# A sum of squared matrix products on one core: one of seven product trees with 20 narrow products, and partial sums that stay in PSUM

## The chip, the cores and the metric

The kernel runs on one core of one Trainium2 chip. The metric is the device time of one execution in microseconds. The trace and its profile page show one execution; the times come from repeated runs without the profiler.

## What is computed

```python
def _L0_rec_ref(x, weight, lin_w, lin_b):      # x 1024x512, weight 64x512x512 (e, f, m), all fp32
    out_lin = x @ lin_w.T + lin_b
    xv = jnp.einsum('bf,efm->bem', x, weight)
    zp = jnp.einsum('bf,efm->bem', jnp.square(x), jnp.square(weight))
    interaction = 0.5 * jnp.sum(jnp.square(xv) - zp, axis=1)
    return out_lin + interaction
```

The large part is `xv`: a 1024x512 matrix times a 512x32768 matrix in fp32, whose result is squared and summed over `e`. The subtracted part needs only the sum over `e` of the squared weights and one small product at the end.

## The kernel before

**Stages.** First comes a prologue: `x` is loaded, the linear part `x @ lin_w.T` is computed (line 369), and the blocks `X1` to `X7` are formed, which are the sums and differences of blocks of `x` that a fast matrix product needs. Then the 512 columns of `m` are worked in groups: two groups of 16 columns of `m` and 20 groups of 24. At the end comes the small product with the summed squares (line 776), and the output is stored.

**A group.** A group is one product of 1024x512 by 512x(24*64) (16*64 in the first two). It is split in two along each of the three dimensions, and 7 outer products take the place of 8 (the Strassen-Winograd scheme); they run in the order 1, 6, 2, 7, 4, 5, 3. Each outer product is a *tree*: it is split in two along each dimension once more and made of 7 inner products, P1 to P7. An inner product is two matmuls (two blocks of 128 rows of `x`) with 384 columns (256 in the first two groups). Each fp32 matmul shows in the trace as two passes, so a tree is 28 passes of 384 columns, each pass with its own weight load.

**PSUM.** There are four pairs of banks: `b1`, `b3`, `b2_0`, `b2_1`. In a tree, P5 goes to `b3` and is copied by ScalarE to SBUF (tile `p5`). P3 is added onto it in `b3` and the sum is copied to SBUF too (tile `p53`). P1 goes to `b1` and is copied by ScalarE to one of the `b2` pairs; P6 is added onto the copy there, then P7, then P4, and the pair is read after each. P2 is added to P1 in `b1`. So four sums come out of a tree, at positions 0 to 3, and two of them also need `p53` or `p5`.

**The outer sums.** `outer_psum` and `outer_sbuf` (lines 518 and 530) add what comes out of PSUM onto the tiles `oa`, `ob` and `c`. In `outer_sbuf`, VectorE first adds bank and `p53` (or `p5`), and a second sum adds this in SBUF to `oa`, `ob` or `c`; that second sum can run on GpSimd or on VectorE. When a block of `xv` is whole, `finish` squares it in place on ScalarE and sums over `e` on VectorE.

**The sums of weights.** Four sums of weight blocks per tree, 128x384 each, are made by GpSimd into tiles `t` (three buffers in turn). GpSimd also issues the accumulating DMAs (line 325) that form `T1`, `T2` and the like. `w_squares` squares the weights on ScalarE and sums them on VectorE.

**The order.** The program is a list of operations with costs. `Plan.order` simulates the engines and fixes the order in which each engine runs its queue. An inner product carries a key: the start of its tree plus `PLACE` times the time of one inner product; among the products that could run, TensorE takes the one with the smallest key. An operation that may run on VectorE or on GpSimd (a sum in SBUF) is taken by VectorE only if it is due within `SPARE` = 15 us.

**The wide tree.** `wide_tree` and `widen` are in the kernel but not used, since `HK` is empty. A wide tree splits an outer product into 4 blocks of rows, 2 of the inner dimension and 3 of columns and takes 20 products in place of 24. Each is one matmul of 256 columns. It uses six single banks as partial sums: `T` and `U` (in `b1` or `b3`), `Q`, `S` (the tree's own `b2` pair), `R`, `V` (the other `b2` pair), with copies by ScalarE from one bank to another between the products.

Of the kernel before, what the change touches and what calls it, by code (L numbers as in the profile page):

```python
# [30 lines left out]
TBUF = 3  # L31
SPARE = 15.0
AHEAD = 20.0
PE, DVE, ACT, POOL, SP = "PE", "DVE", "ACT", "POOL", "SP"

# [5 lines left out]
class Plan:  # L41
# [6 lines left out]

    def add(self, costs, emit, reads=(), writes=(), key=None, land=0.0, both=False):
        op = SimpleNamespace(  # L50
            n=len(self.ops), costs=costs, emit=emit, key=key, land=land,
            deps=set(), succ=[], latest=None, end=None, both=both,
        )
# [128 lines left out]
class Reg:  # L182


    def __init__(self, tile, off, n, *outer):
        self.tile, self.off, self.n, self.outer = tile, off, n, outer
        self.size = n
        offs = [off]
# [8 lines left out]
    @property  # L197
    def ap(self):
        t = self.tile.ap
        free = [list(x) for x in self.outer] + [[1, self.n]]  # L200
        return bass.AP(tensor=t.tensor, offset=t.offset + self.off, ap=[list(t.ap[0])] + free)


@with_exitstack
def kernel(
# [22 lines left out]
    )  # L228
    ps = ctx.enter_context(
        tc.tile_pool(name="ps", bufs=1, space=bass.MemoryType.PSUM)  # L230
    )
    ctx.enter_context(tc.manual_schedule())

    buf = {}

    def make(name, size, pool=sb, unit=SEG):
        t = pool.tile([P, size], F32, tag=name, name=name)
        buf[name] = SimpleNamespace(name=name, ap=t[:, :], unit=unit, size=size, psum=pool is ps)
        return name

    def reg(name, off=0, n=None, *outer):
        t = buf[name]
        return Reg(t, off, t.size - off if n is None else n, *outer)

    def ring(names):
# [19 lines left out]
    for name in ("b1", "b3", "b2_0", "b2_1"):  # L265
        make(name, 2 * N, ps, N)
    b2_ring = ring(["b2_0", "b2_1"])
    acc_ring = ring([make(f"acc{k}", NB * max(GROUPS), sb, 4) for k in range(2)])
    make("w2_sum", NK * M, sb, 4)
    make("bias", M)  # L270
# [10 lines left out]
    def tt(o, a, b, sub=False, only=None):  # L281
# [5 lines left out]
        def emit(e):  # L287
            f = engines[e].tensor_sub if sub else engines[e].tensor_add
            f(o.ap, a.ap, b.ap)  # L289

        plan.add({e: c for e, c in costs.items() if only in (None, e)}, emit,
                 a.atoms + b.atoms, o.atoms, both=not psum)

    def copy(o, i, negative=False):
        def emit(_):
            if negative:
                nc.scalar.activation(o.ap, i.ap, AF.Copy, scale=-1.0)
            else:
                nc.scalar.copy(o.ap, i.ap)  # L299

        plan.add({ACT: 0.19 + 0.00083 * o.size}, emit, i.atoms, o.atoms)

# [28 lines left out]
    def mm(o, x, w, start, key):  # L331
# [6 lines left out]
            ],  # L338
            sum((r.atoms for r in (*x, w, *o)), ()), sum((r.atoms for r in o), ()), key=key,
        )  # L340

# [19 lines left out]
    for k in range(NK):  # L361
        q, r = divmod(k, KH)
        for g, bank in enumerate(lin_banks):
            x = x_in(g // 2, q, r)
            w = reg("ob", KH * H + k * M, M)

            def emit(_, k=k, g=g, bank=bank, x=x, w=w):
                for j in range(2):
                    nc.tensor.matmul(  # L369
                        reg(bank, j * N, N).ap, x.ap[:, ts((g * 2 + j) % (NB // 2), P)], w.ap,  # L370
                        start=(k == 0), stop=(k == NK - 1),
                    )

            plan.add({PE: 2 * mm_cost(N)}, emit, x.atoms + w.atoms, reg(bank).atoms,
                     key=-1000 + 4 * k + g)
    for g, bank in enumerate(lin_banks):
        name, off = ("c", g * 2 * M) if g < 3 else ("w22b", 0)
        for j in range(2):
            tt(reg(name, off + j * M, M), reg(bank, j * N, N), reg("bias"))
        o = reg(name, off, 2 * M)  # L380
# [106 lines left out]
    def tree(time, g, i):  # L487
# [57 lines left out]

        b2, p5, p53 = b2_ring(), p5_ring(), p53_ring()
# [16 lines left out]
    def wide_tree(time, g, i, fresh_bank):  # L563
# [9 lines left out]
        def twice(x):  # L573
            return Reg(x.tile, x.off, x.n, (0, 2))

# [15 lines left out]
        for o, a, b, sub in sums:  # L591
# [7 lines left out]
        aux = "b2_1" if main == "b2_0" else "b2_0"  # L599
        bank = {"T": (fresh, 0), "U": (fresh, 1), "Q": (main, 0), "S": (main, 1),  # L600
                "R": (aux, 0), "V": (aux, 1)}
        cost = mm_cost(V)

        def h(b, half=None):
            name, k = bank[b]
            return reg(name, k * N, 2 * V) if half is None else reg(name, k * N + half * V, V)

# [35 lines left out]
        product(17, "U", 0, True)  # L643
        copy(Reg(h("Q").tile, h("Q").off, V, (V, 2)), twice(h("U", 0)))
        product(10, "T", 1, True)
# [124 lines left out]
    out_dst = out.rearrange("(n p) m -> p n m", p=P)  # L770
    for g, bank in enumerate(("b3", "b1", "b2_0", "b2_1")):
        h = g // 2
        for j in range(2):
            def emit(_, bank=bank, g=g, h=h, j=j):
                for k in range(NK):
                    nc.tensor.matmul(  # L776
                        reg(bank, j * N, N).ap,
                        view(xe[h, k // KH])[:, k % KH, ts((g * 2 + j) % (NB // 2), P)],
                        reg("w2_sum", k * M, M).ap,
                        start=(k == 0), stop=(k == NK - 1),  # L780
                    )

            plan.add({PE: 4 * mm_cost(N)}, emit,
                     xe[h, 0].atoms + xe[h, 1].atoms + reg("w2_sum").atoms,
                     reg(bank, j * N, N).atoms, key=1e6 + 2 * g + j)
            o = Reg(acc_all[g].tile, j * M, M)
            tt(o, reg(bank, j * N, N), Reg(lin_all[g].tile, j * M, M))
            dma(out_dst[:, g * 2 + j, :], o.ap, o.atoms, ())

    for op, engine in plan.order():  # L790
        if op.emit:
            op.emit(engine)

# [32 lines left out]
```

## Time and profile before

| | |
|---|---|
| runs | 1440.97 us median of 3 (1438.86 to 1448.26) |
| profiled execution | 1446.54 us, of which the span of the trace is 1444.8 us |
| TensorE | 1422.6 us busy, 98% of the span, 4440 passes |
| VectorE | 1101.6 us busy, 76% |
| ScalarE | 786.4 us busy, 54% |
| GpSimd | 1149.3 us busy, 80% |

PE is TensorE's matmuls, PEld its weight loads, DVE VectorE, ACT ScalarE, POOL GpSimd; SP's queue issues the plain DMAs. Busy time is the union of an engine's instructions. Neighbouring instructions of one engine overlap a little in the records, so the distance between two starts is what an engine gives up for one instruction. A row "L289 POOL TENSOR_TENSOR t<-w" is the operation of line 289 that reads `w` and writes `t`; buffer numbers are left out.

### The profile page before, as it was taken

How to read it: one execution, taken by the hardware profiler on the slowest of the kernel's cores; microseconds unless marked ns; L12 is line 12 of the kernel's file. 1: busy time of each engine (PE TensorE's matmuls, PEld its weight loads, DVE VectorE, ACT ScalarE, POOL GpSimd, SP SyncE). 2: the span in 40 equal slices, each digit the busy share in tenths (PEclk: the TensorE clock that was granted, in tenths of full speed). 3: DMA queues.
4: the chain of work that ended last, by engine and by line, in shares of the span. 5: the costliest groups of instructions: out<-in, count | busy, mean ns of one | idle time of the engine just before them, and what ended most of it. 6: DMA issues, size and time to landing. Idle time of an engine off the chain costs nothing.

```text
span 1444.8 us, 14609 instructions
## 1 busy us (share of the span) xinstructions
PE 1422.6 (98%) x4440; PEld 839.8 (58%) x4440; DVE 1101.6 (76%) x1226; ACT 786.4 (54%) x1038; POOL 1149.3 (80%) x995
## 2 busy tenths in 40 slices
PE   8999999999999999999999999999999999999998
PEld 3786555555555555555555555555555555555553
DVE  2888778696968778696967869696877869687785
ACT  1456556464746546464555646474654647465541
POOL 6878688797978879796878879797887979788771
PEclk9999999999999999999999999999999999999999
DMA  7666545364555446455454536455544645554242
GB/s 237 168 137 169 131 112 134 90 165 102 138 133 123 120 101 164 90 153 118 120 129 112 134 91 164 102 140 133 123 121 101 164 90 153 123 134 110 68 137 73
DMA packets 78894, 184.53 MB, mean 128 GB/s; under 512 B 28064, under 2 KB 29088, under 8 KB 78816
## 3 DMA queue, kind: packets, MB, share of 16 engines
q1 hardware_dynamic: 65488, 115.17, 25.7%
q0 software_dynamic: 12752, 67.38, 25.4%
q10 hardware_dynamic: 576, 1.05, 0.2%
q8 instruction: 37, 0.61, 0.2%
q14 instruction: 41, 0.34, 0.1%
HBM read 127.04 MB, written 6.19 MB: 92 GB/s over the span
## 4 chain that ended last, share of the span: by engine, by line
PE 91%; DVE 4%; issue 2%; DMA 1%; POOL 1%; ACT 0%; DVEq 0%; SPq 0%; POOLq 0%; ACTq 0%
PE b L335 87%; PE b L776 2%; PE b L369 2%; DVE oa L289 1%; DVE acc L314 1%; DVE ob L289 1%; DMA T<-T1a 1%; DMA w<-T 1%; POOL t L289 0%; DVE c L289 0%; DVE X L391 0%; DMA ob<-lin_wT 0%; DVE p L289 0%; ACT p L299 0%; POOL w L325 0%
## 5 line engine op out<-in xcount | busy, mean ns | idle before, releaser
L335 PE MATMUL b<-t,X 128*128 128x384 f32 (+1 forms) x2464 | 825.9, 478 | 2.7 <-ACT p L299 1.3
L335 PEld LDWEIGHTS b<-t,X 128*128 128x128 f32 x2464 | 464.7, 190 | 317.5 <-POOL t L289 11.8
L299 ACT COPY p<-b 128x768 f32<-128x768 f32 (+1 forms) x308 | 239.2, 777 | 329.7 <-PE b L335 306.2
L335 PE MATMUL b<-w,X 128*128 128x384 f32 (+1 forms) x1056 | 370.8, 481 | 6.2 <-ACT p L299 2.2
L335 PEld LDWEIGHTS b<-w,X 128*128 128x128 f32 x1056 | 199.7, 191 | 143.8 <-DVE oa L289 16.5
L289 POOL TENSOR_TENSOR t<-w 128x384 f32<-128x384 f32 (+1 forms) x176 | 173.1, 996 | 35.6 <-PE b L335 32.9
L299 ACT COPY b<-b 128x768 f32<-128x768 f32 (+1 forms) x154 | 117.6, 764 | 147.9 <-PE b L335 145.0
L289 POOL TENSOR_TENSOR t<-w,t 128x384 f32<-128x384 f32 (+1 forms) x176 | 188.1, 1069 | 9.6 <-PE b L335 8.5
L305 ACT ACTIVATE oa<-oa 128x768 f32<-128x768 f32 (+1 forms) x176 | 140.4, 822 | 70.3 <-POOL oa L289 38.4
L314 DVE TENSOR_REDUCE w_sum<-wsq 128x12 f32<-128x768 f32 (+1 forms) x176 | 160.2, 921 | 17.8 <-ACT wsq L305 16.3
L314 DVE TENSOR_REDUCE acc<-oa 128x12 f32<-128x768 f32 (+1 forms) x176 | 158.2, 919 | 0.5 <-ACT oa L305 0.5
L289 DVE TENSOR_TENSOR p<-b,p 128x768 f32<-128x768 f32 (+1 forms) x132 | 122.4, 928 | 26.6 <-PE b L335 26.5
L289 DVE TENSOR_TENSOR ob<-b,p 128x768 f32<-128x768 f32 (+1 forms) x44 | 41.1, 933 | 116.0 <-PE b L335 112.6
L289 POOL TENSOR_TENSOR ob<-ob,oa 128x768 f32<-128x768 f32 (+1 forms) x40 | 71.8, 1795 | 65.0 <-DVE ob L289 65.0
L305 ACT ACTIVATE wsq<-w 128x768 f32<-128x768 f32 (+1 forms) x132 | 106.8, 826 | 30.1 <-DMA w<-weight 25.3
L289 DVE TENSOR_TENSOR oa<-b,p 128x768 f32<-128x768 f32 (+1 forms) x88 | 81.9, 931 | 23.3 <-PE b L335 23.3
L335 PE MATMUL b<-T,X 128*128 128x384 f32 (+1 forms) x264 | 93.5, 477 | 0.4 <-POOL t L289 0.4
L289 DVE TENSOR_TENSOR ob<-b,oa 128x768 f32<-128x768 f32 (+1 forms) x44 | 41.1, 934 | 64.7 <-PE b L335 62.4
L289 POOL TENSOR_TENSOR c<-c,oa 128x768 f32<-128x768 f32 (+1 forms) x43 | 78.5, 1826 | 9.6 <-DVE c L289 9.5
L289 POOL TENSOR_TENSOR ob<-p,ob 128x768 f32<-128x768 f32 (+1 forms) x43 | 76.5, 1779 | 10.3 <-DVE p L289 10.3
L289 POOL TENSOR_TENSOR oa<-oa,ob 128x768 f32<-128x768 f32 (+1 forms) x44 | 84.0, 1909 | 0.1
L305 ACT ACTIVATE ob<-ob 128x768 f32<-128x768 f32 (+1 forms) x88 | 72.4, 825 | 16.8 <-DVE ob L289 11.6
(85 smaller groups left out, 1651.6 us busy)
## 6 DMA issues: line engine op xcount, KB each, us to landing
w<-weight SPq DMA_DIRECT2D x120, 384.0 KB, 3.7
T<-weight SPq DMA_DIRECT2D x40, 384.0 KB, 4.4
w<-T POOLq DMA_DIRECT2D x20, 768.0 KB, 6.0
T1a<-weight SPq DMA_DIRECT2D x20, 384.0 KB, 4.3
w22a<-weight SPq DMA_DIRECT2D x20, 384.0 KB, 3.4
T1a<-weight POOLq DMA_DIRECT2D x10, 768.0 KB, 7.0
T<-T1a POOLq DMA_DIRECT2D x10, 768.0 KB, 6.0
T1b<-weight SPq DMA_DIRECT2D x20, 384.0 KB, 5.2
```

What stands on the lines that cost most here:

```text
L289: f(o.ap, a.ap, b.ap)
L299: nc.scalar.copy(o.ap, i.ap)
L305: lambda _: nc.scalar.activation(o.ap, i.ap, AF.Square), i.atoms, o.atoms)
L314: nc.vector.tensor_reduce(o, x, axis=AX.X, op=ALU.add)
L335: nc.tensor.matmul(a.ap, b.ap, w.ap, start=start, stop=True, skip_group_check=True)
L369: nc.tensor.matmul(reg(bank, j * N, N).ap, x.ap[:, ts((g * 2 + j) % (NB // 2), P)], w.ap, start=(k == 0), stop=(k == NK - 1),)
L776: nc.tensor.matmul(reg(bank, j * N, N).ap, view(xe[h, k // KH])[:, k % KH, ts((g * 2 + j) % (NB // 2), P)], reg("w2_sum", k * M, M).ap, st ...
```

## The change

- Outer product 1 of the 20 groups of 24 runs as a wide tree (`HK = (1,)`); `widen(1)` makes its 20 blocks of `X1` once, before the first of these groups.
- In the trees of products 6, 2, 7, 4 and 3 (`HOLD`) the sum of P5 and P3 isn't copied to `p53`. It stays in `b3`, and VectorE adds both banks, one after the other, onto the target (two sums with a PSUM input). The inner products of these trees have other places (`HPLACE`). This holds in all 22 groups.
- `SPARE` = -99: VectorE takes no sum that GpSimd can do. `APART`: the plan starts no GpSimd operation beside one of VectorE's sums in SBUF, and none of these beside a running GpSimd operation.
- Two of a tree's four sums of weights, `t1` and `t3`, become one GpSimd instruction over 768 columns.
- Each bank is also a tensor of its own, at the same address as its half of the pair. Wide trees and the small products use the single banks, trees the pairs; `follow` adds the waits between the two views.

```diff
-HK = ()
+HK = (1,)
 PLACE = {5: -6, 3: -2, 1: 0, 6: 3, 2: 4, 7: 6, 4: 9}
+HOLD = (6, 2, 7, 4, 3)
+HPLACE = {5: -1, 1: 0, 3: 1, 6: 2, 2: 3, 4: 11, 7: 5}
-SPARE = 15.0
+SPARE = -99.0
+APART = True
...
+            if APART and e == POOL and free[DVE] > now + 0.1 and running[DVE].both:
+                return None
...
+                if APART and o.both and e == DVE and free[POOL] > now + 0.1:
+                    continue
...
+        base = nc.psum_base
+        pair = nc.alloc_psum_tensor(name, [P, 2 * N], F32).ap()
+        top, nc.psum_base = nc.psum_base, base
+        banks = [nc.alloc_psum_tensor(f"{name}_{k}", [P, N], F32).ap() for k in "lr"]
...
-        for o, a, b in ((t[1], b12, b11), (t[2], b22, t[1]), (t[3], b22, b12), (t[4], b21, t[2])):
+        tt(reg(tn, 0, n, (2 * n, 2)), reg(r, n, n, (2 * n, 2)), reg(r, 0, n, (n, 2)), True, POOL)
+        for o, a, b in ((t[2], b22, t[1]), (t[4], b21, t[2])):
             tt(o, a, b, True, POOL)
+        hold = i in HOLD
...
-               rhs[p], first, time + PLACE[p] * pair)
+               rhs[p], first, time + (HPLACE if hold else PLACE)[p] * pair)
...
+            elif hold and p is None:
+                a, o = part(ADDEND[i], pos), part(TARGET[i], pos)
+                tt(o, whole(bank), a)
+                tt(o, o, whole("b3"))
+                if i in (2, 4, 3):
+                    end(TARGET[i], pos)
...
-        copy(small(p53), whole("b3"))
+        if not hold:
+            copy(small(p53), whole("b3"))
...
+    def follow(op, engine, made):
+        for at, write, alone in op.banks:
+            before = [written[at]] if at in written else []
+            for other, was_alone, insts in before + (read[at] if write else []):
+                if was_alone != alone and not (engine == other == PE):
+                    for x in made:
+                        for y in insts:
+                            tc.add_manual_dep(x.ins, y.ins.name, wait, reason="view of a bank")
...
```

More of the change, by code (lines that the diff above doesn't have):

```diff
@@ L47, in __init__, with add @@
         self.readers = defaultdict(list)
-    def add(self, costs, emit, reads=(), writes=(), key=None, land=0.0, both=False):
+    def add(self, costs, emit, reads=(), writes=(), key=None, land=0.0, both=False,
+            banks=()):
         op = SimpleNamespace(
             n=len(self.ops), costs=costs, emit=emit, key=key, land=land,
-            deps=set(), succ=[], latest=None, end=None, both=both,
+            deps=set(), succ=[], latest=None, end=None, both=both, banks=banks,
         )
@@ L182, with __init__ @@
 class Reg:
-    def __init__(self, tile, off, n, *outer):
+    def __init__(self, tile, off, n, *outer, alone=False):
         self.tile, self.off, self.n, self.outer = tile, off, n, outer
+        self.alone = alone
         self.size = n
@@ L198, in ap, with banks @@
     def ap(self):
-        t = self.tile.ap
+        t, off = self.tile.ap, self.off
+        if self.alone:
+            t, off = self.tile.banks[off // self.tile.unit], off % self.tile.unit
         free = [list(x) for x in self.outer] + [[1, self.n]]
-        return bass.AP(tensor=t.tensor, offset=t.offset + self.off, ap=[list(t.ap[0])] + free)
+        return bass.AP(tensor=t.tensor, offset=t.offset + off, ap=[list(t.ap[0])] + free)
+    def banks(self, written):
+        return tuple((a, written, self.alone) for a in self.atoms) if self.tile.psum else ()
 @with_exitstack
@@ L265 @@
     for name in ("b1", "b3", "b2_0", "b2_1"):
-        make(name, 2 * N, ps, N)
+        base = nc.psum_base
+        pair = nc.alloc_psum_tensor(name, [P, 2 * N], F32).ap()
+        top, nc.psum_base = nc.psum_base, base
+        banks = [nc.alloc_psum_tensor(f"{name}_{k}", [P, N], F32).ap() for k in "lr"]
+        assert nc.psum_base == top
+        buf[name] = SimpleNamespace(name=name, ap=pair, banks=banks, unit=N, size=2 * N, psum=True)
     b2_ring = ring(["b2_0", "b2_1"])
-    acc_ring = ring([make(f"acc{k}", NB * max(GROUPS), sb, 4) for k in range(2)])
-    make("w2_sum", NK * M, sb, 4)
+    acc_ring = ring([make(f"acc{k}", NB * max(GROUPS), 4) for k in range(2)])
+    make("w2_sum", NK * M, 4)
     make("bias", M)
@@ L296, in emit @@
             if negative:
[L297 to L301, printed above, removed]
+                return nc.scalar.activation(o.ap, i.ap, AF.Copy, scale=-1.0)
+            return nc.scalar.copy(o.ap, i.ap)
+        plan.add({ACT: 0.19 + 0.00083 * o.size}, emit, i.atoms, o.atoms,
+                 banks=i.banks(False) + o.banks(True))
     def square(o, i):
@@ L339, in mm @@
             sum((r.atoms for r in (*x, w, *o)), ()), sum((r.atoms for r in o), ()), key=key,
+            banks=sum((r.banks(True) for r in o), ()),
         )
@@ L362, with emit @@
         q, r = divmod(k, KH)
-        for g, bank in enumerate(lin_banks):
+        for g, b in enumerate(lin_banks):
             x = x_in(g // 2, q, r)
             w = reg("ob", KH * H + k * M, M)
-            def emit(_, k=k, g=g, bank=bank, x=x, w=w):
-                for j in range(2):
+            o = [bank(b, j) for j in range(2)]
+            def emit(_, k=k, g=g, o=o, x=x, w=w):
+                return [
                     nc.tensor.matmul(
-                        reg(bank, j * N, N).ap, x.ap[:, ts((g * 2 + j) % (NB // 2), P)], w.ap,
+                        o[j].ap, x.ap[:, ts((g * 2 + j) % (NB // 2), P)], w.ap,
                         start=(k == 0), stop=(k == NK - 1),
                     )
-            plan.add({PE: 2 * mm_cost(N)}, emit, x.atoms + w.atoms, reg(bank).atoms,
-                     key=-1000 + 4 * k + g)
-    for g, bank in enumerate(lin_banks):
+                    for j in range(2)
+                ]
+            plan.add({PE: 2 * mm_cost(N)}, emit, x.atoms + w.atoms, reg(b).atoms,
+                     key=-1000 + 4 * k + g, banks=o[0].banks(True) + o[1].banks(True))
+    for g, b in enumerate(lin_banks):
         name, off = ("c", g * 2 * M) if g < 3 else ("w22b", 0)
         for j in range(2):
-            tt(reg(name, off + j * M, M), reg(bank, j * N, N), reg("bias"))
+            tt(reg(name, off + j * M, M), bank(b, j), reg("bias"))
         o = reg(name, off, 2 * M)
@@ L544, in outer_sbuf @@
                     end(TARGET[i], pos)
-        b2, p5, p53 = b2_ring(), p5_ring(), p53_ring()
+        b2, p5, p53 = b2_ring(), p5_ring(), None if hold else p53_ring()
         product(5, "b3", True)
@@ L573, in twice @@
         def twice(x):
[L574 removed]
+            return Reg(x.tile, x.off, x.n, (0, 2), alone=x.alone)
         tn = t_ring()
@@ L643, in wide_tree @@
         product(17, "U", 0, True)
-        copy(Reg(h("Q").tile, h("Q").off, V, (V, 2)), twice(h("U", 0)))
+        copy(Reg(h("Q").tile, h("Q").off, V, (V, 2), alone=True), twice(h("U", 0)))
         product(10, "T", 1, True)
@@ L770, with emit @@
     out_dst = out.rearrange("(n p) m -> p n m", p=P)
[L771 removed]
+    for g, b in enumerate(("b3", "b1", "b2_0", "b2_1")):
         h = g // 2
         for j in range(2):
[L774 to L775 removed]
+            z = bank(b, j)
+            def emit(_, z=z, g=g, h=h, j=j):
+                return [
                     nc.tensor.matmul(
[L777 to L778 removed]
+                        z.ap, view(xe[h, k // KH])[:, k % KH, ts((g * 2 + j) % (NB // 2), P)],
                         reg("w2_sum", k * M, M).ap,
@@ L781, in emit @@
                     )
+                    for k in range(NK)
+                ]
             plan.add({PE: 4 * mm_cost(N)}, emit,
                      xe[h, 0].atoms + xe[h, 1].atoms + reg("w2_sum").atoms,
-                     reg(bank, j * N, N).atoms, key=1e6 + 2 * g + j)
+                     z.atoms, key=1e6 + 2 * g + j, banks=z.banks(True))
             o = Reg(acc_all[g].tile, j * M, M)
-            tt(o, reg(bank, j * N, N), Reg(lin_all[g].tile, j * M, M))
+            tt(o, z, Reg(lin_all[g].tile, j * M, M))
             dma(out_dst[:, g * 2 + j, :], o.ap, o.atoms, ())
+    wait = mybir.DependencyInfo(mybir.DependencyClass.Sync, mybir.DependencyReason.DATA)
+    written, read = {}, defaultdict(list)
+    def follow(op, engine, made):
[6 more added lines that the diff above has]
+                            tc.add_manual_dep(x.ins, y.ins.name, wait, reason="view of a bank")
+        for at, write, alone in op.banks:
+            if write:
+                written[at], read[at] = (engine, alone, made), []
+            else:
+                read[at].append((engine, alone, made))
     for op, engine in plan.order():
         if op.emit:
-            op.emit(engine)
+            made = op.emit(engine)
+            if op.banks:
+                follow(op, engine, made if isinstance(made, list) else [made])
 def kernel(r_x, L0_rec_weight, L0_rec_lin_w, L0_rec_lin_b):
```

22 lines of the change are left out of this document (11 added, 11 removed).

## The prediction

> **What bounds the kernel now.** I read the page first (busy times, chain), then the waits of TensorE in the long middle part, then busy time by stretch.
>
> ```profile
> span 1444.8 us, 14609 instructions
> PE 1422.6 (98%) x4440; PEld 839.8 (58%) x4440; DVE 1101.6 (76%) x1226; ACT 786.4 (54%) x1038; POOL 1149.3 (80%) x995
> ...
> PE 91%; DVE 4%; issue 2%; DMA 1%; POOL 1%; ACT 0%; DVEq 0%; SPq 0%; POOLq 0%; ACTq 0%
> ...
> engine line waited for: us in total, times, longest us
> PE b L335 <- ACT p L299: 2.2, 1, 2.2
> ...
> core 0: us, PE busy (x) PEld busy (x) DVE busy (x) ACT busy (x) POOL busy (x), PEclk, DMA share, GB/s
> 55.00:140.00 85.00, 80.39 (x344) 65.22 (x343) 70.28 (x104) 49.47 (x85) 70.19 (x79) 0.98 0.61 151
> 400.00:600.00 200.00, 199.69 (x617) 116.09 (x616) 150.99 (x165) 112.42 (x145) 162.14 (x136) 1.00 0.51 123
> 600.00:800.00 200.00, 197.52 (x604) 114.44 (x603) 153.43 (x164) 110.87 (x143) 160.74 (x135) 0.99 0.50 120
> ```
>
> TensorE is the bound: 98% of the span, 91% of the chain, and between 200 and 1390 us (the waits row) it waited once, 2.2 us. So time can come only from fewer passes, from that one wait, and from the 16-column groups, where some 5 of 85 us are idle. And every wait that the change adds at TensorE shows in full.
>
> **Fewer passes.** The pace of 384 and of 256 columns, from a group of 24 and a group of 16:
>
> ```profile
> 563.82 4.03 PE L335 MATMUL b<-t,X 128*128 128x384 f32 x12
> 567.69 1.45 PE L335 MATMUL b<-T1a,X 128*128 128x384 f32 x4
> ...
> 86.34 2.75 PE L335 MATMUL b<-t,X 128*128 128x256 f32 x12
> 88.93 1.03 PE L335 MATMUL b<-w,X 128*128 128x256 f32 x4
> ...
> L335 PEld LDWEIGHTS b<-t,X 128*128 128x128 f32 x2464 | 464.7, 190 | 317.5 <-POOL t L289 11.8 <-issue 9.1 <-DVE p L289 8.6
> ```
>
> Twelve passes take 3.87 us at 384 columns (0.3225 each) and 2.59 us at 256 (0.2158). A tree has 14 matmuls, 28 passes, 9.03 us; a wide tree 20 matmuls, 40 passes, 8.63 us. The weight load of 0.19 us still fits under a pass of 0.2158, as it does in the 16-column groups. Saved: 0.40 us in each of 20 groups, **7.9 us**. It is the whole gain that the arithmetic offers, 0.55%.
>
> **VectorE's sums in SBUF go.** Here is where the one long wait comes from:
>
> ```profile
> 701.01 5.90 DVE L289 TENSOR_TENSOR ob<-ob,p 128x768 f32<-128x768 f32 x1
> 707.00 0.80 ACT L299 COPY p<-b 128x768 f32<-128x768 f32 x1 [3.83 <-DVE ob L289]
> 707.86 2.93 PE L335 MATMUL b<-w,X 128*128 128x384 f32 x4 [2.17 <-ACT p L299]
> 710.58 1.80 PE L335 MATMUL b<-t,X 128*128 128x384 f32 x4
> ...
> L289 DVE TENSOR_TENSOR ob<-ob,p 128x768 f32<-128x768 f32 x19 | 41.8, 2199 | 0.0
> L289 DVE TENSOR_TENSOR oa<-p,oa 128x768 f32<-128x768 f32 x20 | 19.2, 959 | 2.1
> L289 POOL TENSOR_TENSOR ob<-ob,p 128x768 f32<-128x768 f32 x21 | 39.4, 1877 | 5.3 <-DVE p L289 5.3
> ```
>
> One and the same sum takes VectorE 0.96 us with GpSimd quiet and 2.2 us beside it, and once 5.90 us, while GpSimd ran sums back to back. ScalarE's copy waited behind that one, and TensorE behind the copy. Then four passes took 2.72 us (707.86 to 710.58) where they take 1.29. The stretch 600 to 800 has 604 passes where 400 to 600 has 617: 13 passes, **4.2 us**, of which 2.2 are the wait and the rest slow passes behind it. The change sends these sums to GpSimd, so the event can't happen again. But it belongs to this one execution: the profiled 1446.5 us lie 5.6 above the median of the runs, whose lowest is 2.1 below the median. A median run can hold at most about those 2.1 us of such events; I take 1.0.
>
> [...]
>
> **Load of the engines per group of 24.** VectorE: five HOLD trees each get one more sum with a PSUM input (0.95 us long, 0.87 apart), two sums in SBUF go, and tree 1's two sums of 768 become two of 512 and four of 256.
>
> ```profile
> L289 DVE TENSOR_TENSOR p<-b,p 128x768 f32<-128x768 f32 x120 | 114.2, 952 | 24.9 <-PE b L335 24.9
> L289 DVE TENSOR_TENSOR p<-b,p 128x512 f32<-128x512 f32 x12 | 8.2, 685 | 1.6 <-PE b L335 1.6
> L299 ACT COPY b<-b 128x768 f32<-128x768 f32 x140 | 109.6, 783 | 139.1 <-PE b L335 139.1
> L299 ACT COPY b<-b 128x512 f32<-128x512 f32 x14 | 8.0, 571 | 8.8 <-PE b L335 5.9 <-DVE c L289 1.0 <-DVE oa L289 0.8
> L289 POOL TENSOR_TENSOR t<-w 128x384 f32<-128x384 f32 x160 | 158.9, 1005 | 31.1 <-PE b L335 30.2 <-POOL t L289 0.8
> L289 POOL TENSOR_TENSOR ob<-p,ob 128x512 f32<-128x512 f32 x3 | 3.8, 1273 | 0.2 <-DVE p L289 0.2
> L289 POOL TENSOR_TENSOR t<-w 128x256 f32<-128x256 f32 x16 | 14.2, 910 | 4.5 <-PE b L335 2.6 <-DMA w<-T 1.9
> ```
>
> A step of 256 columns is worth 0.27 us on VectorE and 0.21 on ScalarE, so I estimate 0.41 and 0.36 for 256. VectorE: +4.4 -3.2 -1.7 +2.9 = +2.4 us on 48 (76% of 63.2; it becomes 80%). ScalarE: -5 x 0.80 for the copies to `p53`, and tree 1's five copies (4.0) become six of 512 and five of 256 (5.2): -2.8. GpSimd: twelve outer sums become nine (-5.5); 28 sums of weights (28) become six trees of one 768 sum (as `ob<-ob,p`, 1.88) and two of 384 (23.3), and wide sums of 4 x 1.27 + 4 x 0.91 = 8.7: +4.0. In all -1.5. No engine becomes the bound by its load. What's left are waits at single places.
>
> **HOLD trees: shorter turns through ScalarE.** By `HPLACE` P5, P1, P3, P6 stand in a row, so that one product (1.29 us) lies between P5 and P3 and between P1 and P6, where the old places leave several; P3 must wait until P5 is copied, P6 until P1 is. The end of the program shows a turn with one product between:
>
> ```profile
> 1408.98 2.74 PE L335 MATMUL b<-t,X 128*128 128x384 f32 x8
> 1409.18 0.78 ACT L299 COPY b<-b 128x768 f32<-128x768 f32 x1 [3.02 <-PE b L335]
> 1410.02 1.09 PEld L335 LDWEIGHTS b<-t,X 128*128 128x128 f32 x4 [0.20 <-ACT b L299]
> ```
>
> The copy began 0.20 us after the product, and the load for the next one waited for it, yet the eight passes ran without a gap (2.74 us is 8 x 0.3225 plus the end of the last). 1.04 us from product to load, 0.19 for the load, 1.29 to hide it: it fits by 0.06 us if ScalarE is free. If a square is in its way (0.84 us) up to 0.8 is lost, in 110 trees up to 86 us; but P4 of the tree before (key 11) is at hand to fill, which gives 0. A gain is excluded: TensorE waited for such a copy only once. The copies to `p53` would be free of cost anyway, since ScalarE is busy 54%; their going gives it room. `b3` is now held until VectorE's second sum, some 2.1 us after P6; P5 of the next tree comes three products later. I take the end at 0, with **1 us** in all.
>
> **The wide tree's own turns.** Three: 17 is copied to `Q` before 19 and 7 (cover 0.86 us, two products; needed 0.20 + 0.57 + 0.25 = 1.02); 3, a VectorE sum and a copy to `V` before 11 (cover 2.2, needed 1.7); 2 and the reads of `S` before 13 (cover 0.86, needed 1.1 or more). Uncovered that is 0.4 us per tree, 8 us in all, the same as the saving; covered by P4 of tree 3 and P5, P1, P3 of tree 6, which have other banks, it's 0. The fillers are four products (5 us), so I stay near 0: **1.5 us**.
>
> **GpSimd ahead of the wide tree.** Rows of one group, from outer product 5 to 1:
>
> ```profile
> 566.24 1.97 POOL L289 TENSOR_TENSOR t<-w 128x384 f32<-128x384 f32 x2
> ...
> 569.01 1.82 POOL L289 TENSOR_TENSOR oa<-oa,p 128x768 f32<-128x768 f32 x1
> 570.79 1.82 POOL L289 TENSOR_TENSOR ob<-ob,p 128x768 f32<-128x768 f32 x1
> 572.87 1.81 POOL L289 TENSOR_TENSOR oa<-oa,p 128x768 f32<-128x768 f32 x1 [0.27 <-DVE p L289]
> ...
> 578.01 1.45 PE L335 MATMUL b<-w,X 128*128 128x384 f32 x4
> ```
>
> Most of tree 1's sums were made here (up to 568) before tree 5's additions (569 on), and the fourth of these additions was one of the VectorE sums that go. After: their buffer `t` is free only once tree 4's P4 has run, two products later than before (key 11 for 9), so the wide sums (8.7 us) meet four additions (7.3) between 569 and tree 1's start: P3 at 578.0, P1 two products later, at 580.6, where product 17 would stand. That is 16.0 us of work in 11.6: 4.4 us late, if the additions go first; 0 if those to `oa`, which tree 1 writes only some 5 us after its start, go behind. Behind a late sum stand the wide tree's products and then tree 6's, which share its banks. The plan orders by due time, so I stay near 0: **1.5 us** over 20 groups.
>
> **The rest.** In the prologue two sums of 1024 and the 13 operations of `widen` (some 7 us) come to GpSimd, in the narrow groups HOLD trims its work; the transitions' waits are between operations that depend on each other anyway. I take 0 for these, between -3 and +4.
>
> **The sum.** Against the profiled execution (1446.5, 1.7 outside the span): 1446.5 - 7.9 - 4.2 + 1 + 1.5 + 1.5 = 1438.4. Against the median, which is 5.6 lower and holds less of the stall: 1440.97 - 7.9 - 1.0 + 4.0 = 1436.1. I predict **1436**, and 1431 to 1441 for this case.
>
> **Rivals.** (a) *The gain comes whole*: the turns all hide, and the narrow groups win back 2 of their 5 us: 1441 - 7.9 - 1 - 2 = 1430. For it: TensorE had one wait in 1190 us. Against: the shorter cover. (b) *Slower: GpSimd late for the wide tree.* One mechanism: TensorE stands at product 17 or 10 of tree 1 until its sums are there. It decides from 0.45 us per group (20 x 0.45 = the gain of 8.9). At 1.3 us it gives 1441 - 8.9 + 26 = 1458. Waits of 2 us also bring slow passes behind them, as at 707.86. For it: the 16 us above, and no more help by VectorE. Against: 80% average load, falling. [...] (c) *HOLD's copies meet a busy ScalarE*: 110 trees x 0.15 = 16, so 1441 - 8.9 + 16 = 1448. (d) *No shorter pace*: in the wide tree every second pass carries a wait, so loads stop running ahead: 40 x (0.19 + 0.06) = 10.0 us, 1.0 more than a tree, +20: 1441 - 1 + 20 = 1460. Against: the narrow groups' pace.
>
> **How the numbers follow.** Forecast 0.50, (a) 0.20, (b) 0.18, (c) 0.08, (d) 0.04. A measurement here can tell about 1%, 14.4 us, from no change. Faster by more needs 1426.6: a fifth of (a), 0.04. Slower by more needs 1455.4: two thirds of (b), a quarter of (c), three quarters of (d), 0.17. Within 1%: 0.79. The range runs from 1428 (every cost 0, 2.1 of waits gone and 3 won back: 1441 - 7.9 - 2.1 - 3) to 1456 ((b) at 1.2 us per group).
>
> **What would show it.** Right: 240 more passes (12 in each of 20 trees), those of tree 1 at about 0.216 us; groups of 24 some 62.8 us apart instead of 63.2; no VectorE sum `ob<-ob,p`; copies `p<-b` of 768 down from 280 to 140 (five HOLD trees lose one each, tree 1 two); waits of TensorE in the middle part of some 4 us in all. Wrong: TensorE waiting on `POOL t` at each tree 1 (b), on `ACT p` or `ACT b` in the HOLD trees (c), passes of 256 at 0.25 (d).

## The result and the profile after

| | before | after |
|---|---|---|
| median of the runs | 1441.09 us (4 runs, 1438.86 to 1448.26) | 1426.93 us (4 runs, 1426.46 to 1427.61) |
| profiled execution | 1446.54 us, span 1444.8 | 1427.20 us, span 1425.4 |

The ratio of the times is 0.9894, with an interval of 0.9859 to 0.9928: the change makes the kernel 14.2 us faster. The forecast was 1436 with a range of 1428 to 1456, so the kernel came out 9 us faster than forecast and 1.1 us below the range.

The page of after, its busy times and the chain:

```profile
span 1425.4 us, 14830 instructions
...
PE 1407.8 (99%) x4680; PEld 883.2 (62%) x4680; DVE 1123.7 (79%) x1365; ACT 731.2 (51%) x1048; POOL 1093.3 (77%) x895
...
PE 91%; DVE 6%; issue 1%; DMA 1%; POOL 1%; ACT 0%; SPq 0%; DVEq 0%; POOLq 0%
```

There are 240 passes more, in 14.8 us less of TensorE's time. VectorE is up by 22 us and GpSimd down by 56, and neither is near its bound. The stretches of after, in the columns of the prediction's table:

```profile
core 0: us, PE busy (x) PEld busy (x) DVE busy (x) ACT busy (x) POOL busy (x), PEclk, DMA share, GB/s
...
55.00:140.00 85.00, 84.34 (x370) 68.68 (x369) 70.50 (x112) 50.19 (x87) 77.33 (x82) 1.00 0.65 158
400.00:600.00 200.00, 200.00 (x660) 124.42 (x659) 162.78 (x193) 106.69 (x150) 156.49 (x123) 1.00 0.54 129
600.00:800.00 200.00, 199.83 (x659) 124.06 (x658) 163.30 (x195) 107.33 (x151) 158.38 (x127) 1.00 0.54 128
```

TensorE is busy throughout, and in the stretch of the narrow groups (55 to 140) 80.39 us have become 84.34, with 26 more passes. What TensorE waited for between 36 and 140 us, first before (the three longest rows of six) and then after (engine, line, releaser: us in total, times, longest):

```profile
PE b L335 <- DVE ob L289: 2.3, 3, 1.1
PE b L335 <- DMA w<-T: 2.0, 1, 2.0
PE b L335 <- ACT p L299: 1.3, 2, 0.8
```

```profile
PE b L356 <- DVE oa L309: 0.3, 1, 0.3
PE b L356 <- POOL t L309: 0.2, 1, 0.2
```

**A ledger from pass to pass.** The waits view is not enough for the long middle part. Here is one group of before, in order of time:

```profile
230.18 0.94 DVE L314 TENSOR_REDUCE acc<-oa 128x12 f32<-128x768 f32 x1
...
230.41 1.53 PE L335 MATMUL b<-t,X 128*128 128x384 f32 x4
...
231.04 0.95 DVE L289 TENSOR_TENSOR oa<-b,ob 128x768 f32<-128x768 f32 x1
...
232.04 0.94 PEld L335 LDWEIGHTS b<-w,X 128*128 128x128 f32 x4 [0.72 <-DVE oa L289]
232.04 1.56 PE L335 MATMUL b<-w,X 128*128 128x384 f32 x4
```

Four passes at 0.3225 us from 230.41 end at 231.70, yet the next begin at 232.04: the product waited for VectorE to read its bank (231.04 + 0.95 us). PE's row shows no wait, because its modelled end (230.41 + 1.53) covers most of it; only the row of the weight load shows one. Ahead of that read VectorE had a reduction to finish (230.18). The wait comes again in each group. TensorE's waits of before list nothing for it; those of the weight loads, between 200 and 1390 us, do:

```profile
PEld b L335 <- DVE oa L289: 12.9, 18, 0.7
```

So I went through all pass starts of both traces and took from each distance to the next start what a pass needs by the prediction's pace (0.3225 us at 384 columns, 0.2158 at 256, others in proportion). The rest is lost time:

| us of the profiled execution | before | after | difference |
|---|---|---|---|
| passes at their pace | 1403.3 | 1395.4 | -7.9 |
| lost, 0 to 36 (prologue) | 2.8 | 2.7 | 0.0 |
| lost, 36 to 140 (narrow groups) | 12.1 | 4.3 | -7.7 |
| lost, 140 to 1300 | 13.9 | 5.8 | -8.2 |
| lost, 1300 to the end | 0.9 | 6.0 | +5.2 |

With 0.7 us less behind the last pass that is the 19.3 us between the two profiled executions. Of the 13.9 us, 4.1 are the event at 705 to 711 and some 4.8 the wait of 0.27 us in 18 groups. Three passes close to that wait take 0.07 to 0.10 us longer than the pace, so that the place costs 0.51 us a group, 9.2 of the 9.8 us that are not the event. The loss at the end differs between executions: a second profile of after has 4.2 us there. Without the event the difference is 15.2 us, against 14.2 between the medians.

### The profile page after: what moved, and what is told of

It is laid out like the page before. It is cut to its first block, busy times and chain, and to the rows that moved or that the text cites. A ratio compares the mean times of both kernels' runs of the same rounds, so it can differ in the third digit from the quotient of the medians.

```text
span 1425.4 us, 14830 instructions
## 1 busy us (share of the span) xinstructions
PE 1407.8 (99%) x4680; PEld 883.2 (62%) x4680; DVE 1123.7 (79%) x1365; ACT 731.2 (51%) x1048; POOL 1093.3 (77%) x895
## 4 chain that ended last, share of the span: by engine, by line
PE 91%; DVE 6%; issue 1%; DMA 1%; POOL 1%; ACT 0%; SPq 0%; DVEq 0%; POOLq 0%
PE b L356 75%; PE b_r L356 6%; PE b_l L356 6%; DVE acc L335 1%; DVE ob L309 1%; PE b_l L393 1%; DVE oa L309 1%; PE b_r L393 1%; PE b_l L813 1%; PE b_r L813 1%; DVE p L309 1%; DVE w_sum L335 1%; DMA X<-xT 1%; DVE c L309 0%; DMA ob<-lin_wT 0%
## 5 line engine op out<-in xcount | busy, mean ns | idle before, releaser
L356 PE MATMUL b<-t,X 128*128 128x384 f32 (+1 forms) x2144 | 720.9, 476 | 5.1 <-DVE oa L309 3.3
L356 PEld LDWEIGHTS b<-t,X 128*128 128x128 f32 x2144 | 403.2, 190 | 266.9 <-issue 23.2
L356 PE MATMUL b<-w,X 128*128 128x384 f32 (+1 forms) x816 | 276.1, 474 | 0.0
L309 POOL TENSOR_TENSOR t<-w 128x768 f32<-128x768 f32 (+1 forms) x128 | 182.4, 1431 | 119.7 <-PE b_l L356 104.4
L319 ACT COPY p<-b 128x768 f32<-128x768 f32 (+1 forms) x158 | 122.3, 774 | 173.4 <-PE b L356 173.2
L309 POOL TENSOR_TENSOR ob<-ob,p 128x768 f32<-128x768 f32 (+1 forms) x44 | 78.8, 1791 | 22.9 <-DVE p L309 22.9
L326 ACT ACTIVATE c<-c 128x768 f32<-128x768 f32 (+1 forms) x88 | 70.4, 819 | 47.9 <-DVE c L309 46.6
L309 POOL TENSOR_TENSOR t<-t,w 128x256 f32<-128x256 f32 (+1 forms) x80 | 90.2, 1202 | 0.0
L309 DVE TENSOR_TENSOR oa<-oa,b 128x768 f32<-128x768 f32 (+1 forms) x88 | 81.2, 923 | 0.8
L309 DVE TENSOR_TENSOR ob<-ob,b 128x768 f32<-128x768 f32 (+1 forms) x88 | 80.0, 926 | 2.0 <-PE b L356 1.4
```

Source lines behind the costliest of these rows:

```text
L309: return f(o.ap, a.ap, b.ap)
L319: return nc.scalar.copy(o.ap, i.ap)
L326: lambda _: nc.scalar.activation(o.ap, i.ap, AF.Square), i.atoms, o.atoms)
L356: nc.tensor.matmul(a.ap, b.ap, w.ap, start=start, stop=True, skip_group_check=True)
```

## The experiments

The first four runs undo parts of the change, and later ones take the order of the queues apart. Every kernel was timed in three rounds against the kernel before on the same chip (1439.35, 1442.93, 1441.54 and 1441.59 us in the four sets). The lost time is that of the one profiled execution of each kernel. All times:

| kernel | median us | ratio, interval | lost 36-140 | 140-1300 | 1300-end |
|---|---|---|---|---|---|
| after, once more | 1426.67 | 0.9894, 0.9852-0.9936 | 4.3 | 5.8 | 4.2 |
| no wide tree | 1472.07 | 1.0223, 1.0199-1.0247 | 9.3 | 39.2 | 4.5 |
| no HOLD | 1439.60 | 0.9994, 0.9981-1.0007 | 10.8 | 15.8 | 4.6 |
| VectorE's sums back | 1433.23 | 0.9951, 0.9935-0.9967 | 6.5 | 12.0 | 3.5 |
| all three undone | 1447.47 | 1.0049, 1.0034-1.0064 | 11.1 | 19.0 | 1.2 |
| wide tree alone | 1461.66 | 1.0140, 1.0104-1.0176 | 4.4 | 42.2 | 3.8 |
| GpSimd alone for the sums | 1444.87 | 1.0020, 1.0003-1.0037 | 5.2 | 14.5 | 4.8 |
| HOLD in groups of 24 only | 1428.82 | 0.9913, 0.9884-0.9942 | 6.1 | 6.3 | 3.3 |
| later landing, all DMAs | 1437.74 | 0.9964, 0.9943-0.9984 | 5.6 | 20.5 | 1.1 |
| the same, no wide tree | 1478.80 | 1.0253, 1.0215-1.0290 | 4.2 | 51.4 | 4.5 |
| lag 5, no wide tree | 1427.31 | 0.9901, 0.9878-0.9924 | 4.2 | 3.6 | 1.0 |
| lag 5, after | 1436.28 | 0.9970, 0.9958-0.9982 | 8.9 | 17.4 | 0.6 |
| lag 5, before | 1443.02 | 1.0009, 0.9996-1.0022 | 8.3 | 9.8 | 2.2 |
| lag 10, after | 1423.78 | 0.9874, 0.9859-0.9889 | 6.3 | 5.7 | 0.8 |
| lag 10 and a shorter HOP | 1422.96 | 0.9870, 0.9855-0.9885 | 5.0 | 6.5 | 0.8 |
| two wide trees, lag 5 | 1419.22 | 0.9841, 0.9824-0.9858 | 7.6 | 7.0 | 1.6 |

**No wide tree.**

```diff
-HK = (1,)
+HK = ()
```

> The changed kernel with HK empty: no wide trees, all else as changed. Theory A (the edits add up: 7.9 us are the shorter passes of 20 wide trees, some 7.7 us come from the narrow groups through HOLD, the rest from the VectorE sums that went): 1426.9 + 7.9 = 1434.8 us, with no new waits of TensorE between 140 and 1300 us. Rival B (the wide tree also moves waits, by easing or loading ScalarE and GpSimd): outside 1433 to 1437.

The wide tree was worth 7.9 us of passes; without it the kernel takes 45 us more, far from the 1434.8 of theory A. The waits of TensorE between 200 and 1390 us, and a stretch of one group:

```profile
PE b L356 <- DVE p L309: 24.1, 19, 1.7
```

```profile
509.13 0.84 ACT L326 ACTIVATE wsq<-w 128x768 f32<-128x768 f32 x1 [3.03 <-DMA w<-weight]
...
510.01 0.95 DVE L335 TENSOR_REDUCE w_sum<-wsq 128x12 f32<-128x768 f32 x1 [2.46 <-ACT wsq L326]
510.88 0.95 DVE L309 TENSOR_TENSOR p<-b,p 128x768 f32<-128x768 f32 x1
...
511.88 1.56 PE L356 MATMUL b<-t,X 128*128 128x384 f32 x4 [1.46 <-DVE p L309]
```

Read from the bottom: TensorE waits 1.46 us for a bank that VectorE has yet to read; VectorE stands behind a reduction; the reduction waits for ScalarE's square; and the square, at the head of ScalarE's queue, waited 3.03 us for a weight that had not landed. None of these rows belongs to the removed trees: the plan made another order, this one puts a square too early, and the order repeats, so the wait comes in 19 groups.

**No HOLD; VectorE's sums back; all three undone.** One diff each:

```diff
-HOLD = (6, 2, 7, 4, 3)
+HOLD = ()
```

```diff
-SPARE = -99.0
-APART = True
+SPARE = 15.0
+APART = False
```

The third takes both of these and `HK = ()`; what is left of the change are the joined sums of weights and the single banks.

> The changed kernel with HOLD empty: P5+P3 is copied to SBUF again in all trees and the old places hold. Theory A (HOLD frees the narrow groups): the waits of TensorE between 36 and 140 us come back, some 1434 us. Rival C (what counted is that no sum in SBUF runs on VectorE any more, HOLD does nothing by itself): 1428 us or less. If GpSimd, with five more outer sums per group, becomes late: above 1436, with TensorE or VectorE waiting for GpSimd.

> The changed kernel with SPARE = 15 and APART off: VectorE may take sums in SBUF again. Theory A (those sums cost only the rare long wait): 1428 to 1430 us, and a wider spread of the runs. Rival C (their sharing with GpSimd is what cost the time): 1434 to 1440.

> All three off (HK and HOLD empty, SPARE = 15, APART off); what is left of the change is the joined pair of sums of weights and the single banks. All theories: near the kernel before, 1439 to 1443 us. If the joined sums alone matter (GpSimd gets some 0.15 us per tree back): 1435 to 1438.

Against after's 1426.67, 12.9 us of the gain go without HOLD. The time lies where the third case of the expectation has it, but the cause is another: TensorE waits in nearly every group for VectorE's read of a bank, not for GpSimd.

```profile
PE b L356 <- DVE oa L309: 4.0, 19, 0.3
```

All three undone came out 4.5 us above the range that all theories gave. With VectorE's sums back 6.6 us go (between the two ranges of its expectation), 6.2 of them in the middle part, though these sums are quick here:

```profile
L309 DVE TENSOR_TENSOR oa<-oa,p 128x768 f32<-128x768 f32 x19 | 20.5, 1078 | 0.0
L309 DVE TENSOR_TENSOR ob<-ob,p 128x768 f32<-128x768 f32 x19 | 17.9, 943 | 0.0
```

```profile
PE b_r L356 <- DVE ob L309: 3.0, 18, 0.2
```

The first view is the sums' mean time (1.08 and 0.94 us), the second TensorE's wait. It is one wait per group for VectorE's reading of a bank; the pass starts make it 0.33 us each. So what this run lost is not the longer sums that the prediction looked at (2.2 us each in before; the median is 1.99, as the event's 5.90 is in that mean). Nor did the sums themselves make VectorE late: in the group that I followed, the last of them ran at 563.19, and VectorE then stood idle twice for TensorE (1.04 us before 565.17, 0.43 before 566.56) ahead of the read that the wide tree waited for at 569.29. The same wait of 0.33 us ahead of the wide tree comes in 4 of 18 groups of after, and in 17 or 18 in two orders further down (later landing, and lag 5), with no such sum on VectorE. It belongs to the order; that these sums bring it isn't shown.

**Two parts alone.** `HOLD = ()` with `SPARE = 15.0` and `APART = False` leaves the wide tree alone; `HK = ()` with `HOLD = ()` leaves GpSimd alone for the sums.

> Only the wide trees (HOLD empty, SPARE = 15, APART off; joined sums and single banks stay). Theory A (edits add up): 7.9 us below the run with all three off, 1439 to 1440. Rival F (order decides): 3 us or more away from that, to either side.

> Only the sums in SBUF on GpSimd alone (HK and HOLD empty). Theory A (VectorE's share of these sums is what cost 6 us in the run with VectorE's sums back): 6 us below the run with all three off, 1441 to 1442. Rival G (GpSimd, with 14 outer sums per group, becomes late without HOLD): above 1447, with TensorE or VectorE behind GpSimd.

With the four runs above, the wide tree's effect can be read in three surroundings: about +14 us on all three undone (1447.47 to 1461.66), -5 on GpSimd alone (1444.87 to 1439.60), and -45 beside HOLD and GpSimd alone (1472.07 to 1426.67). The two kernels of a pair ran in different sets, whose kernel before differed by up to 3.6 us; by the ratios the three are +13, -4 and -47, so the -5 is uncertain in size. The passes save 7.9 us in each. The parts don't add up; what differs is the wait that each order repeats. In the wide tree alone the pass starts show 0.79, 0.72 and 0.33 us lost in nearly every group, and its waits of TensorE name the first two:

```profile
PE b_r L356 <- ACT b_l L319: 11.3, 18, 0.6
PE b L356 <- ACT oa L319: 10.0, 18, 0.6
```

These are the wide tree's own copies by ScalarE, so the turns that the prediction priced at 1.5 us can cost far more, in another order than after's. GpSimd alone (1444.87) met neither its theory A nor its rival G.

**HOLD in the groups of 24 only.**

```diff
-        hold = i in HOLD
+        hold = i in HOLD and GROUPS[g] == max(GROUPS)
```

> HOLD in the 20 groups of 24 only; the two groups of 16 run their trees as before. Theory A (the narrow groups won their 7 us through HOLD): TensorE's lost time between 36 and 140 us comes back, +4 to +7, 1431 to 1434 us. Rival C (they won it by GpSimd alone doing the sums, and by the joined sums): 1426 to 1428.

It costs 2.2 us against after in the same set (1426.67), nearer to rival C than to theory A. HOLD in the narrow groups is therefore at most a small part of the 7.7 us won there. Over the orders above, the time lost there runs from 4.3 to 11.1 us and follows no one part: 4.4 with the wide tree alone, 5.2 with GpSimd alone, 10.8 with these two together. How the 7.7 us split is open.

**Is it the landing of the loads?** First for all plain DMAs, then for the squares alone. `land` is what the plan adds to a DMA's time in its queue before the data count as there.

```diff
-    def dma(o, i, reads, writes, cost=2.4, land=1.5, queue=nc.sync):
+    def dma(o, i, reads, writes, cost=2.4, land=4.5, queue=nc.sync):
...
-        dma(view(x), x_src[:, ts(q, KH), ts(h, H)], (), x.atoms)
+        dma(view(x), x_src[:, ts(q, KH), ts(h, H)], (), x.atoms, land=6.0)
```

> The changed kernel, with the plan's allowance from the end of a plain DMA's queue time to its landing raised from 1.5 to 4.5 us (6.0 for the reload of x at the end), nothing else. Theory D (the end of the changed kernel loses 5 us because VectorE's queue stands behind a reload of x that lands later than planned, and behind it TensorE): the wait of 2.8 us for VectorE's oa near 1361 goes, 1422 to 1425 us. Rival E (with later loads in the plan other queues get worse, or the wait comes from VectorE's load): 1426 or more.

> No wide trees (HK empty), with the same larger allowance for landings. Theory D (no_wide was 45 us slower because once per group ScalarE waited for a weight that had not landed, VectorE's reduction for ScalarE, VectorE's read of a bank behind that, TensorE behind the read; the wide trees as such are worth only their passes): the 2 us per group go, 7.9 us above the changed kernel with the same allowance, 1431 to 1435 us. Rival B (wide trees relieve more than the passes, their narrow reads for instance): stays above 1445.

The second is the same with `HK = ()`. Both were slower than without the edit, by 11 and 7 us. At the end the first lost 1.1 us in place of 4 to 6, as theory D has it, but its middle part lost 20.5, as rival E has it. Without the wide tree ScalarE's squares still stood behind loads:

```profile
ACT wsq L326 <- DMA w<-weight: 83.1, 38, 4.1
```

There the edit did not keep the squares from their loads, so it does not decide on theory D for the middle part. The next one delays only the squares, and the sum that folds the reloaded `x` into `X`:

```diff
-            return max([0.0] + [d.end for d in o.waits]) + self.HOP
+            return max([0.0] + [d.end + (o.lag if d.land else 0.0) for d in o.waits]) + self.HOP
...
-                 lambda _: nc.scalar.activation(o.ap, i.ap, AF.Square), i.atoms, o.atoms)
+                 lambda _: nc.scalar.activation(o.ap, i.ap, AF.Square), i.atoms, o.atoms, lag=5.0)
...
-            x.atoms, x.atoms,
+            x.atoms, x.atoms, lag=5.0,
```

> No wide trees (HK empty), and in the plan alone the squares of freshly loaded weights (and the squares of the reloaded x) count as ready 5 us after the planned landing of their transfer; no other operation's allowance changes. Theory D (no_wide loses 2 us per group because ScalarE's queue stands behind a square whose weight hasn't landed): the waits of ScalarE for weights fall from some 70 us to under 15, TensorE's two waits per group go, 1432 to 1438 us. Rival B (without wide trees the HOLD order is worse by itself): above 1455, with the waits at other places.

> The changed kernel with the same 5 us for squares of fresh weights and for the reloaded x. Theory D: the wait of 2.8 us near the end (VectorE behind the reload of x) goes and nothing else gets worse: 1421 to 1425 us. Rival F (any change of the plan shuffles all queues, and the small waits per group come and go with it): 1428 to 1440, with a new wait repeated in each group.

> The kernel before, with only the plan's 5 us for squares of fresh weights and for the reloaded x. If the order alone explains the gain (rival F in its strong form): 1430 or less. If HOLD and the sums on GpSimd alone are what lets TensorE run with almost no waits (theory H: VectorE's and ScalarE's queues have a wait per group in the kernel before that no order removes): 1437 to 1443, with a wait of TensorE of about 0.3 us in every group still.

Without the wide tree, 1472 us became 1427.3. ScalarE's waits for a weight load, over the whole span, first without and then with the lag:

```profile
ACT wsq L326 <- DMA w<-weight: 84.1, 41, 3.3
```

```profile
ACT wsq L328 <- DMA w<-weight: 1.3, 1, 1.3
```

TensorE's wait went with them, and the time fell below the 1432 of theory D. That supports the chain from load to square to reduction to bank; the lag also reorders the rest, so it doesn't test the chain alone. But a delay that cures one order does not better another by itself: after with the lag took 1436.3, with two waits of 0.37 and 0.33 us in each group, and before with the lag took 1443.0, which is no change. Its wait of 0.27 us per group stayed; the weight loads of before with the lag, 200 to 1390 us:

```profile
PEld b L337 <- DVE oa L291: 12.9, 18, 0.7
```

So an order almost free of waits was found with HOLD and the sums on GpSimd together, and not in the kernel before. Whether one of the two is enough with the lag wasn't tried.

**The wait that goes with HOLD.** One wait doesn't change with the order. In the group of before shown above, VectorE's read at 231.04 is that of tree 7's P2 from `b1`, and the product at 232.04 is tree 4's P1, which overwrites `b1`. In each of the six kernels without HOLD (before, lag 5 before, no HOLD, all three undone, wide tree alone, GpSimd alone) the pass starts show such a wait, with VectorE's `oa` as releaser, in all 18 groups between 140 and 1300 us, 0.27 to 0.41 us long. In none of the twelve traces with HOLD does it come. Whether the other places do it (`HPLACE` puts P2 earlier) or the copy that is gone wasn't tried.

**Towards a better version.** The lag of 10 us for the squares (5 for `x`); the same with `HOP` 0.15 in place of 0.18; and products 1 and 3 as wide trees with the lag of 5:

```diff
-HK = (1,)
+HK = (1, 3)
```

> The changed kernel with wide trees in product 1; squares of fresh weights count as ready 10 us after the planned landing, the reloaded x 5 us after. Theory H: waits between 140 and 1300 us as small as in the changed kernel, the 3 us at the end gone, 1421 to 1425 us; with waits as small as in no_wide_lag it would be 1427.3 - 7.9 = 1419. Rival F: 1430 or more with a wait repeated in each group.

> As lag10, with the plan's allowance for a handover between engines at 0.15 us instead of 0.18. Theory H: within 3 us of lag10. Rival F: more than 5 us away from it.

> Wide trees in products 1 and 3, 5 us for squares of fresh weights and the reloaded x. Passes: 40 trees x 0.40 = 15.9 us less than seven plain trees. Theory H: 1427.3 - 15.9 = 1411 with waits as small as in no_wide_lag, and some 5 to 8 us above it for one or two small waits per group: 1412 to 1420. Rival B (wide trees cost as much in waits as they save in passes): 1425 or more.

Lag 10 wins back the end (0.8 us lost there in place of 4 to 6): 1423.8. The shorter `HOP` adds nothing that can be told apart. Two wide trees give 1419.2 us, the best of all, 7.7 us below after and 22 below before in its set. From its page:

```profile
span 1417.1 us, 15723 instructions
...
PE 1401.1 (99%) x4920; PEld 929.0 (66%) x4920; DVE 1123.4 (79%) x1446; ACT 766.9 (54%) x1148; POOL 1227.4 (87%) x1087
```

## Why the prediction was wrong, step by step

- **Fewer passes: right.** 240 more passes came, and the ledger has 7.9 us less. The wide tree of the group whose first products start at 628.77:

```profile
630.56 1.03 PE L356 MATMUL b_l<-t,X 128*128 128x256 f32 x4
631.42 1.03 PE L356 MATMUL b_r<-t,X 128*128 128x256 f32 x4
632.29 0.59 PE L356 MATMUL b_r<-w,X 128*128 128x256 f32 x2
```

  Eight passes in 1.73 us, 0.216 each, so rival (d), loads that no longer fit, is out. Wide trees begin 62.96 us apart (502.85, 565.81, 628.77); the groups of before were 63.75 apart, not the 63.2 that the prediction took; 0.51 of that difference is the wait with the slower passes beside it.

- **What bounds the kernel: the step that failed first.** "It waited once, 2.2 us" was read from PE's row, whose modelled ends hid the wait of 0.27 us in each of 18 groups. The time lost between 140 and 1300 us was 13.9 us, and 9.8 without the event; so there was more to win than the event.

- **The three costs (1 + 1.5 + 1.5): the sign was wrong, by HOLD.** The turns and GpSimd ahead of the wide tree were to cost 4.0 us. Against the 9.8, after lost 5.8: 4.1 us won. The step that failed is "A gain is excluded: TensorE waited for such a copy only once". It looked only at products behind ScalarE's copies; HOLD took away a wait behind VectorE's read of `b1`, worth 0.51 us in each group with the slower passes beside it, and the new order gave back some of that. HOLD's turns and the wide tree's turns left no wait that comes in every group, nor did rivals (b) and (c). All waits of TensorE in after from 200 to 1390 us:

```profile
PE b L356 <- DVE oa L309: 3.0, 2, 2.8
PE b L356 <- DVE ob L309: 1.3, 4, 0.6
PE b_r L356 <- DVE ob L309: 0.7, 4, 0.2
```

  They are 5.0 us where some 4 were forecast, but that is luck: 2.8 of it is a single wait at the end, and neither `POOL t` nor an ACT tile is among the releasers. For (b), the rows show why: most of the wide tree's sums are made ahead of the additions that the prediction let go first:

```profile
612.50 2.24 POOL L309 TENSOR_TENSOR t<-t,w 128x512 f32<-128x512 f32 x2
...
616.20 1.54 POOL L309 TENSOR_TENSOR t<-t,w 128x512 f32<-128x512 f32 x1
618.83 1.83 POOL L309 TENSOR_TENSOR ob<-ob,p 128x768 f32<-128x768 f32 x1 [1.10 <-DVE p L309]
620.61 3.60 POOL L309 TENSOR_TENSOR oa<-oa,p 128x768 f32<-128x768 f32 x2
...
628.77 0.59 PE L356 MATMUL b_r<-t,X 128*128 128x256 f32 x2
```

  Sums of 512 columns are the wide tree's; they are done by 618, and the additions after them are over before the tree starts at 628.77. The estimates of 0.41 and 0.36 us for 256 columns on VectorE and ScalarE came out at 0.42 and 0.38:

```profile
L309 DVE TENSOR_TENSOR oa<-b_r,p 128x256 f32<-128x256 f32 x60 | 25.3, 422 | 35.2 <-PE b_r L356 33.2 <-ACT oa L319 1.2 <-ACT p L319 0.4
L319 ACT COPY p<-b_r 128x256 f32<-128x256 f32 x40 | 15.2, 380 | 11.3 <-PE b_r L356 10.9 <-DVE oa L309 0.4
L319 ACT COPY p<-b 128x768 f32<-128x768 f32 x140 | 111.8, 799 | 162.1 <-PE b L356 162.1
```

  The copies `p<-b` of 768 are down from 280 to 140, as forecast.

- **VectorE's sums (1.0): open.** The event at 701 didn't come again. The run with the sums back lost 6.6 us, but by a wait that other orders have without these sums, so what the sums are worth beyond the event stays open.

- **The rest (0, between -3 and +4): two terms, both mis-sized.** The narrow groups gave 7.7 us, where 5 were thought idle and at most 3 to be won. The end cost 5.2 us. Its main wait, in after:

```profile
1357.30 1.45 PE L356 MATMUL b<-t,X 128*128 128x384 f32 x4
...
1357.78 1.97 DVE L779 SCALAR_TENSOR_TENSOR X<-X 128x1024 f32<-128x1024 f32 x1 [4.27 <-DMA X<-xT]
...
1360.54 1.81 DVE L309 TENSOR_TENSOR oa<-b,ob 128x768 f32<-128x768 f32 x2
...
1361.53 1.56 PE L356 MATMUL b<-t,X 128*128 128x384 f32 x4 [2.78 <-DVE oa L309]
```

  VectorE stood 4.27 us behind the reload of `x` for the last product, with the bank read behind it; a row that the prediction did not look for.

- **The sum.** Forecast: 7.9 + 1.0 - 4.0 = 4.9 us. Found, by the ledger without the event: 7.9 + 7.7 + 4.1 - 5.2 + 0.7 = 15.2, with the medians at 14.2. So the two terms that failed most are the narrow groups, put at 0, and the three costs, put at -4.0. HOLD's part of the second is shown by eighteen traces; how the narrow groups' 7.7 us came about is open. Beyond HOLD's wait, what the prediction priced edit by edit is a property of the order: most runs above have waits of their own, at one or two places of a group, and a wait w costs some 20 w.

## What to carry to other kernels

In a kernel whose order is fixed and repeated, price an edit by the order that it makes: a wait of 0.3 us at one place of a group was 6 us here, and the wide tree changed the time by about -45, -5 or +14 us in three surroundings. To tell an edit's own effect from that of the order, look for a wait that comes and goes with the edit in several orders, as HOLD's does. Look for such waits in the distances between TensorE's starts and in the rows of its weight loads; the rows of the matmuls hid the one of 0.27 us in before. When an engine's queue waits for a load, follow what is queued behind: the operation that uses the load need not be urgent for its wait to reach TensorE.

## What the runs showed of the hardware

**Slow passes after a wait.** Behind a wait of 3.41 us the kernel without HOLD ran at half its pace: eight passes took 3.42 us (46.74 to 50.16), 0.43 each where 0.216 is the pace. The granted clock (the third column from the right) between 45 and 50 us was 0.50:

```profile
44.88 2.08 PE L356 MATMUL b<-t,X 128*128 128x256 f32 x4 [3.41 <-DVE oa L309]
46.74 3.62 PE L356 MATMUL b<-T,X 128*128 128x256 f32 x8
50.16 3.06 PE L356 MATMUL b<-t,X 128*128 128x256 f32 x12
```

```profile
45.00:50.00 5.00, 5.00 (x12) 4.01 (x13) 1.70 (x3) 1.44 (x3) 2.96 (x4) 0.50 0.48 180
```

In before, the clock was 0.61 between 707 and 711 us and 0.57 between 110 and 114, behind waits of 2.17 and 2.04 us:

```profile
707.00:711.00 4.00, 3.14 (x5) 1.85 (x6) 4.00 (x5) 1.82 (x3) 1.34 (x1) 0.61 0.26 84
110.00:114.00 4.00, 3.32 (x8) 2.73 (x9) 0.95 (x1) 1.41 (x2) 3.39 (x5) 0.57 0.71 241
```

In finer steps it was 0.50 from 110.53 to 113.94 and from 707.86 to 711.27, and 1.00 in the 3 us before and after each. But the prediction's "Waits of 2 us also bring slow passes behind them" does not hold for every such wait. In after, the clock stayed at 1.00 around the wait of 2.78 us that ends at 1361.53, and through the whole stretch from 12 to 1424 us:

```profile
1361.00:1366.00 5.00, 4.21 (x12) 2.30 (x13) 5.00 (x7) 1.61 (x2) 4.32 (x4) 1.00 0.51 184
```

Why the clock fell behind the two shorter waits and not behind this one is not shown: no run was made to test it.
